# Three placements in a queued schedule: masks behind the token sums, bias preparation last, a longer pause ahead of the scaling

## The chip, the cores and the metric

The kernel runs on one core of a Trainium2 chip. The time is the device time of one execution in microseconds (us). The kernel before takes 2967.13 us (median of three runs, 2965.59 to 2967.64). A trace is one execution, and the same kernel's runs differ by 1 to 5 us, so a difference of a microsecond between two traces is not by itself an effect. The "granted clock" in the traces is the share of TensorE's full clock that it was given (1.00 is all of it).

## The reference, cut to what matters

```python
h = relu(layernorm(x))
for l in range(2):
    u_left, u_right = (h @ (h @ W[l].T).T / sqrt(768) for W in (W_left, W_right))
    u = u_left * triu(adj) + u_right * triu(adj, 1).T          # the masks
    e = exp(u) * adj
    attention = e / (e.sum(-1) + 1e-10)
    h_lin = h @ W_lin[l].T + b_lin[l]                          # bias, centred ahead of time
    h = relu(layernorm_ddof1(attention @ h_lin) * a[l] + b[l]) # "scaling" of tokens
x = x + h
```

There are 128 graphs of 64 tokens, 768 features, in fp32. The kernel works through them in 16 blocks of 512 tokens, in two passes per layer.

## The kernel before

A block of pass one consists of six projections (left and right weights, three column groups). Each projection is computed by seven products of six matmuls (a Strassen-like scheme), into the banks X, Y, Z and V of PSUM (the memory into which this kernel's matmuls write; here a bank is read out before it is used anew). The products read the tokens `ht`, four sums of tokens `ts` (T1 to T4, made by GpSimd), and sums of weights. After each product, one piece of side work is taken from a queue:

```python
def pump(n):
    for _ in range(n):
        f = queue.popleft() if queue else None
        if f is None and idle:
            f = idle.popleft()          # an empty piece gives a turn to the idle work
        if f is not None:
            f()
```

What a block does for the next one, and what it leaves to the end:

```python
def prepare(u):
    transpose_rows(l, u, sp)                       # norm, transposes, store to DRAM
    queue.append(lambda: load_h(1, l, u))          # ht back from DRAM
    if u + 1 < NB:
        queue.append(lambda: load_rows(l, u + 1, sp))
    queue.extend(softmax(u - 2) if u > 1 else [])
    queue.append(lambda: load_adj(u))              # the adjacency
    queue.extend(none * 6)                         # the pause
    affine(1, l, u)                                # ScalarE scales ht (layer 1 only)
    queue.append(lambda: masks(u))                 # GpSimd: wm <- adj * tri, waits for adj
    sums_t((1, l, u))                              # GpSimd: T1 to T4 of ht
...
late = [queue.pop() for _ in range(2)][::-1]       # T3 and T4
for k in range(2):
    for g in range(CH):
        project(u, k, g, ...)
        if k == g == 0 and u in aside:
            aside[u]()                             # block 1: one_aside
        if k == 1 and g == CH - 2:
            flush()
            queue.extend(none * 3 + late)
```

The idle work of pass one is started in each layer's second block (`u == 1`):

```python
def one_aside(l):
    def begin():
        load_w(l, "n")      # four weight loads: A11, A21, A22, A12
        bias(l)             # two loads at once; its VectorE piece goes into the idle work
        centre(l)           # idle: 2 empty, mean of A11 and A21 (VectorE), subtractions (GpSimd), ...
        sums_w(l, "n", nc.gpsimd, idle, 2)
    return begin
```

In the traces VectorE, ScalarE, GpSimd and the load queue execute their instructions in program order: one that waits holds those behind it (T1 at 80.03 us, behind masks that started at 78.67). The queue therefore decides what stands in front of what on VectorE, ScalarE, GpSimd and the load queue.

## Time and profile before

| | before |
|---|---|
| time, median | 2967.13 us |
| TensorE busy | 2906.3 us, 98% |
| waits of TensorE that the change can touch | 31.0 us |
| layer 0, second and third block | 71.48 and 61.89 us |
| layer 1, first and second block | 59.32 and 80.39 us |
| a block without a gap | 59.98 us |

The block times run from the first product of a block (X, left weights) to that of the next. They are the right unit here, because a wait of TensorE costs more than its own length. The lines behind this table are in the prediction below.

### The profile page before, as it was taken

What the parts mean: (1) busy time and instruction counts of PE and PEld (TensorE: products, weight loads), DVE (VectorE), ACT (ScalarE), POOL (GpSimd) and SP (SyncE); (2) the same over time, 40 slices, a digit from 0 to 9 for tenths busy, and PEclk for the clock granted to TensorE, in tenths of its full rate; (3) what the DMA queues carried; (4) which work ended last, traced back from release to release, by engine and by line L of the source; (5) the groups of instructions that cost most, each with busy time, mean ns of one, the idle gap of its engine ahead of it and who ended that gap; (6) DMA issues with size and microseconds to landing.
All of it is one profiled execution on the core that took longest, in us unless ns stands there. A gap on an engine that the chain in (4) does not pass through costs nothing.

```text
span 2965.4 us, 37443 instructions
## 1 busy us (share of the span) xinstructions
PE 2906.3 (98%) x14872; PEld 2243.7 (76%) x14872; DVE 1128.6 (38%) x2316; ACT 582.6 (20%) x1113; POOL 754.4 (25%) x478
## 2 busy tenths in 40 slices
PE   8899999999999999999997999999999999999998
PEld 7788888888888655555586888888888886555554
DVE  5444334443343232222333333333333324555555
ACT  2112111211121122222211111111111112232221
POOL 0231111111211262322312211111111114656564
PEclk9999999999999999999998999999999999999999
DMA  6423432243222243332443342234223303554544
GB/s 191 115 70 81 115 83 70 73 112 94 70 70 72 103 134 120 100 118 94 141 116 94 103 104 71 70 91 114 74 70 86 101 24 114 169 160 148 177 143 133
DMA packets 228655, 310.23 MB, mean 105 GB/s; under 512 B 53632, under 2 KB 179072, under 8 KB 220288
## 3 DMA queue, kind: packets, MB, share of 16 engines
q1 hardware_dynamic: 228192, 307.05, 37.2%
q8 instruction: 117, 1.92, 0.3%
q10 hardware_dynamic: 288, 0.79, 0.1%
q14 instruction: 58, 0.48, 0.0%
HBM read 202.91 MB, written 104.86 MB: 104 GB/s over the span
## 4 chain that ended last, share of the span: by engine, by line
PE 94%; DMA 3%; DVE 1%; SPq 1%; issue 0%; ACT 0%; POOL 0%; DVEq 0%; ACTq 0%; POOLq 0%
PE Z L326 16%; PE V L326 16%; PE X L326 16%; PE Z L566 8%; PE V L566 8%; PE X L566 8%; PE Y L326 8%; PE aux L360 6%; PE Y L566 5%; PE aux L494 3%; DMA h<-xb 1%; DMA x<-z 1%; DMA x<-in_x_dram 0%; DMA b<-in_b_lin_dram 0%; SPq L273 0%
## 5 line engine op out<-in xcount | busy, mean ns | idle before, releaser
L296 POOL TENSOR_TENSOR wm<-adj,tri 128x256 f32<-128x256 f32 x64 | 46.3, 744 | 1423.9 <-DMA adj<-in_adj_dram 1225.2
L151 POOL TENSOR_TENSOR ts<-ht 128x768 f32<-128x768 f32 x126 | 240.1, 1906 | 284.4 <-PE Y L326 155.4
L326 PE MATMUL X<-ht,w_r_A 128*128 128x256 f32 x1152 | 281.1, 380 | 2.9 <-ACT n L345 2.9
L326 PE MATMUL V<-ts,w_l_A 128*128 128x256 f32 x1152 | 281.1, 380 | 0.0
L326 PE MATMUL X<-ht,w_l_A 128*128 128x256 f32 x1152 | 280.1, 379 | 0.0
L326 PE MATMUL V<-ts,w_r_A 128*128 128x256 f32 x1152 | 280.0, 379 | 0.0
L566 PE MATMUL X<-w_n_A,ht 128*128 128x384 f32 x768 | 268.8, 486 | 0.0
L566 PE MATMUL V<-w_n_A,ts 128*128 128x384 f32 x768 | 268.6, 486 | 0.0
L345 ACT COPY n<-X 128x256 f32<-128x256 f32 x192 | 71.4, 372 | 981.0 <-PE X L326 981.0
L347 DVE TENSOR_TENSOR n<-V,u 128x256 f32<-128x256 f32 x384 | 161.8, 421 | 235.9 <-PE V L326 235.3
L326 PEld LDWEIGHTS X<-ht,w_r_A 128*128 128x128 f32 x1152 | 219.4, 191 | 33.2 <-ACT n L345 3.3
L326 PEld LDWEIGHTS V<-ts,w_l_A 128*128 128x128 f32 x1152 | 219.8, 191 | 30.1
L326 PEld LDWEIGHTS X<-ht,w_l_A 128*128 128x128 f32 x1152 | 218.7, 190 | 30.3 <-issue 0.6
L326 PEld LDWEIGHTS V<-ts,w_r_A 128*128 128x128 f32 x1152 | 218.9, 190 | 29.8
L151 POOL TENSOR_TENSOR ts<-ht,ts 128x768 f32<-128x768 f32 x126 | 238.7, 1894 | 8.4 <-issue 6.0
L566 PEld LDWEIGHTS V<-w_n_A,ts 128*128 128x128 f32 x768 | 145.9, 190 | 101.8
L566 PEld LDWEIGHTS X<-w_n_A,ht 128*128 128x128 f32 x768 | 145.8, 190 | 101.6 <-issue 0.3
L340 DVE TENSOR_TENSOR u<-Y,s 128x256 f32<-128x256 f32 x192 | 81.4, 424 | 369.1 <-PE Y L326 362.1
L520 ACT ACTIVATE z<-aux 128x768 f32<-128x768 f32 x128 | 102.5, 806 | 597.9 <-PE aux L494 583.8
L347 DVE TENSOR_TENSOR n<-Z,u 128x256 f32<-128x256 f32 x192 | 81.4, 424 | 307.3 <-PE Z L326 307.2
L343 DVE TENSOR_TENSOR u<-Z,u 128x256 f32<-128x256 f32 x192 | 81.5, 424 | 280.5 <-PE Z L326 280.1
L337 ACT COPY s<-X 128x256 f32<-128x256 f32 x192 | 71.1, 370 | 587.0 <-PE X L326 586.9
(107 smaller groups left out, 3987.5 us busy)
## 6 DMA issues: line engine op xcount, KB each, us to landing
ht<-h SPq DMA_DIRECT2D x63, 1536.0 KB, 7.0
h<-xb SPq DMA_DIRECT2D x124, 384.0 KB, 6.1
z<-z SPq DMA_DIRECT2D x128, 192.0 KB, 2.9
x<-z SPq DMA_DIRECT2D x128, 192.0 KB, 8.7
xr<-in_x_dram SPq DMA_DIRECT2D x128, 192.0 KB, 3.4
out_dram<-xr SPq DMA_DIRECT2D x128, 192.0 KB, 2.7
x<-in_x_dram SPq DMA_DIRECT2D x120, 192.0 KB, 8.5
adj<-in_adj_dram SPq DMA_DIRECT2D x64, 128.0 KB, 2.8
```

Of the source, the lines that this page charges most:

```text
L151: eng.tensor_sub(b[o], b[m], b[n])
L296: nc.gpsimd.tensor_tensor(WM[u][:, :, k], ADJ[u][:, :, 1 - k], t, op=ALU.mult)
L326: nc.tensor.matmul(p, w[a][:, c, g * P:(g + 1) * P], b[t][:, c, :], start=(new and c == 0), stop=(c == CH - 1), skip_group_check=True)
L337: nc.scalar.copy(s1, p)
L340: nc.vector.tensor_add(u2, p, s1)
L343: nc.vector.tensor_add(u4, p, u2)
L345: nc.scalar.copy(to, pb)
L347: nc.vector.tensor_add(to, pb, (u4 if i == 3 else u2).rearrange("p (b s) -> p b s", s=S))
L360: nc.tensor.matmul(p[h * S:(h + 1) * S, q, :], ht[:, c, b * S:(b + 1) * S], m[c // CH][:, c % CH, b].rearrange("p k j -> p (k j)"), start= ...
L494: nc.tensor.matmul(cx[k][i, m, :HH], at[j, q, :], hl[j, q, m * HH:(m + 1) * HH], start=True, stop=True)
L520: nc.scalar.activation(zs[k].rearrange(two, n=2), cx[k], AF.Square, accum_out=ss[:, k:k + 1])
L566: nc.tensor.matmul(p, b[t][:, c, r * P:(r + 1) * P], w[a][:, c, :], start=(new and c == 0), stop=(c == CH - 1), skip_group_check=True)
```

## The change

The masks had GpSimd wait for the adjacency while the token sums stood behind them; they move to the end of the block. The bias preparation had VectorE wait for the bias; it moves behind the rest of the idle work. The scaling had ScalarE wait for `ht`; the pause ahead of it grows from six to nine empty pieces where a layer's second block is prepared, which happens during its first.

```diff
@@ prepare(u) @@
                 queue.append(lambda: load_adj(u))
-                queue.extend(none * 6)
+                queue.extend(none * (6 if u > 1 else 9))
                 affine(1, l, u)
-                queue.append(lambda: masks(u))
                 sums_t((1, l, u))
@@ end of a block @@
                             flush()
                             queue.extend(none * 3 + late)
+                            if u + 1 < NB:
+                                queue.append(lambda: masks(u + 1))
@@ one_aside(l) @@
             load_w(l, "n")
-            bias(l)
             centre(l)
             sums_w(l, "n", nc.gpsimd, idle, 2)
+            bias(l)
```

## The prediction

> **What bounds the kernel now.** I read the page's busy times first, then who waits for whom on TensorE, then busy time stretch by stretch, and only then the order of time around each wait.
>
> ```profile
> PE 2906.3 (98%) x14872; PEld 2243.7 (76%) x14872; DVE 1128.6 (38%) x2316; ACT 582.6 (20%) x1113; POOL 754.4 (25%) x478
> ```
>
> TensorE is busy 98% of 2965.4 us, and the diff removes no matmul. Only its idle time and its slow time are to be had. The waits of TensorE:
>
> ```profile
> PE Z L326 <- DVE u L343: 17.4, 2, 16.7
> ...
> PE Y L326 <- POOL ts L151: 9.0, 1, 9.0
> PE X L326 <- ACT n L345: 2.9, 1, 2.9
> PE aux L360 <- DVE n L347: 1.7, 1, 1.7
> ```
>
> Columns are total us, times, longest. These four make 31.0 us (the others, 14.1 us, are the start and a pass's edge, untouched). A wait also costs time afterwards, so I take whole blocks, from one block's first product to the next one's. The stretches below are layer 0's second, third and fourth block, then layer 1's first, second and third:
>
> ```profile
> 73.31:144.79 71.48, 62.48 (x349) 54.60 (x348) 29.23 (x67) 10.35 (x19) 14.11 (x11) 0.93 0.45 122
> 144.79:206.68 61.89, 60.23 (x350) 53.02 (x349) 28.57 (x60) 11.42 (x20) 18.46 (x11) 1.00 0.33 83
> 206.68:266.66 59.98, 59.98 (x350) 53.02 (x349) 23.59 (x56) 11.42 (x20) 18.91 (x12) 1.00 0.34 86
> 1478.89:1538.21 59.32, 56.45 (x254) 49.05 (x253) 16.08 (x35) 12.27 (x25) 12.28 (x10) 0.97 0.52 129
> 1538.21:1618.60 80.39, 63.00 (x349) 54.64 (x348) 29.70 (x56) 10.41 (x20) 16.26 (x10) 0.89 0.36 98
> 1618.60:1678.58 59.98, 59.98 (x349) 53.02 (x348) 19.14 (x42) 9.13 (x19) 19.60 (x11) 1.00 0.33 86
> ```
>
> Second column is the stretch, third PE busy, third from the end the granted clock. A full block takes 59.98 us with no gap. A layer's first has no scores (5.39 us in the chain of waits), so 54.59. The excess: 71.48-59.98 = 11.50; 61.89-59.98 = 1.91; 59.32-54.59 = 4.73; 80.39-59.98 = 20.41. In all 38.6 us, 1.3% of the time. That is the ceiling of this change: 2% (59 us) is out of reach.
>
> **What the Trainium skill says.** "Perfetto Trace Analysis", section "Optimization Strategy", says to find the gaps on the engine that limits and what blocks them; here the gaps name POOL, ACT and DVE, each itself held by a transfer. "TensorE: Matmul & The Clock Gate", section "What's actually happening", says that TensorE falls to half clock after an idle window and needs some 3.4 us of work to get back. The trace agrees: six matmuls of one product take 1.46 us in the steady state, after the 9.00 us pause 2.93; even the 2.87 us pause is followed by 2.62 and 2.13. So a wait costs about 2 to 2.6 us beyond its length (11.50-9.00 = 2.5), except one under 2 us (1.91-1.66). "SBUF — State Buffer", section "Who interferes with whom", says that a VectorE instruction with two SBUF inputs, or in a two-port mode, is shut out by a GpSimd instruction for its whole length. The trace agrees: the three-column add and scaling of the weight means take 0.16 and 0.17 us alone, but 1.62 and 1.74 at 146.68 and 148.34, ending where a GpSimd instruction ends (148.28, 150.04).
>
> **The change part by part.** A block runs six projections of seven products, 1.295 us apart (72.01 to 73.31). After each product one piece of the queue is given out; an empty piece takes one from the idle work. Engines work in program order, so a piece that waits for a transfer holds what follows.
>
> *Masks behind the token sums.* Layer 0's second block needs T2 for its second product (Y). In time:
>
> ```profile
> 63.31 0.35 SPq L211 DMA_DIRECT2D ht<-h  x1
> ...
> 73.31 1.46 PE L326 MATMUL X<-ht,w_l_A 128*128 128x256 f32 x6
> ...
> 78.67 1.40 POOL L296 TENSOR_TENSOR wm<-adj,tri 128x256 f32<-128x256 f32 x2 [49.51 <-DMA adj<-in_adj_dram]
> 80.03 1.80 POOL L151 TENSOR_TENSOR ts<-ht 128x768 f32<-128x768 f32 x1
> 81.91 1.80 POOL L151 TENSOR_TENSOR ts<-ht,ts 128x768 f32<-128x768 f32 x1
> ```
>
> The masks wait for the adjacency, and T1 and T2 stand behind them. Their data is there long before: ht is issued at 63.31 and takes 6.8 us to land, so 70.11. Without the masks ahead, T1 and T2 take the 3.7 us they take now (80.03 to 83.71) and end near 73.85; Y would start at 73.31+1.30 = 74.61. Margin 0.75 us. T3 and T4 follow by 77.5, before V needs T3 (some 82.5, behind the scores). All of 11.5 goes. The masks' consumer, the softmax, comes a block later. In the other blocks GpSimd's wait for the adjacency (1225.2 us over 27 waits) is beside TensorE and its end is worth nothing.
>
> *Longer pause.* Only a layer's second block gets nine empty pieces instead of six, given out during the first block. In layer 0 nothing is scaled, and the queue's rest is flushed at the same place, so there it does nothing. In layer 1 ScalarE's scaling waits for ht until 1516.46, and the copy that frees bank X, due at 1512.87, stands behind it until 1517.89. Three pieces later the scaling follows that copy; the next X product starts at its time (1515.26). The next copy then is delayed to about 1518.3, but its bank is needed only at 1520.4. T1 and T2 still end by 1523, needed at about 1535. So 4.7 goes.
>
> *Bias at the end of the idle work.* In layer 1's second block VectorE stands in the bias from 1562.5 to 1582.01, and TensorE stops at 1568.56:
>
> ```profile
> 1569.30 3.00 SPq L100 DMA_DIRECT2D w_n_A<-in_w_lin_dram  x4
> 1572.85 1.19 SPq L450 DMA_DIRECT2D b<-in_b_lin_dram  x2
> ...
> 1582.01 0.55 DVE L460 TENSOR_REDUCE bm<-b 128x1 f32<-128x384 f32 x1 [19.45 <-DMA b<-in_b_lin_dram]
> ...
> 1585.25 2.93 PE L326 MATMUL Z<-ht,w_l_S 128*128 128x256 f32 x6 [16.69 <-DVE u L343]
> ```
>
> But the next idle piece is the weights' mean, and it reads the weights whose loads were issued just ahead of the bias. Counting pieces: the bias had the first empty piece of the third projection; the mean now has the third. VectorE thus writes u (Y) and u (Z) at 1566.5, then waits for the first weight half: issued 1569.30, 7.8 us, lands 1577.1. Reduction 1.34: 1578.4. Second: issued about 1570.05, 8.4 us, lands 1578.45; reduction to 1579.8, two small instructions to 1580.2, then the n (V) write to 1580.6. TensorE can run X and Z meanwhile and stops only at the last V, due at 1569.7, until 1580.65: 10.9 us instead of 16.7. Afterwards two slow products (2.72 and 2.46): that projection's end plus one product is at 1585.8, where it was 1591.7. Saved: 5.9. The later 0.7 us wait (second mean, blocked by GpSimd) goes as the mean gets another place: 0.8. Of 20.4 some 6.7 goes, 13.7 stays, with VectorE's n (V) as the new releaser.
>
> *A cost.* In layer 0's second block the second mean moves from after the last projection's sixth product to after its second. Of the old clock: it starts at 139.0, two reductions to 141.6; GpSimd meanwhile runs T3, T4 and the moved masks (139.8 to 144.8), so each of the two small instructions waits for one of them to end: about 143.4 to 144.2. The u (Z) write then ends near 144.2 and the product Z due at 142.21 is 1.7 to 2.5 us late. The old place cost 1.9; I put the new one at 2.4: 0.5 lost. The bias itself (2.3 us of VectorE) falls in a later block, landed long since, and costs nothing.
>
> Sum: 11.5 + 4.7 + 6.7 - 0.5 = 22.4 us; 2967.1 - 22.4 = 2944.7.
>
> **Rivals.**
> 1. *The bias's wait goes altogether* (the intent): 20.4 goes, about 2931. For: the group was named by the bias. Against: the weights' landing times above.
> 2. *The mean inherits the whole wait*, because it effectively waits for all four weight loads: the last, issued 1571.95, takes 9.5 us and lands at 1581.4; the saving is about 3 and the time 2948.5. Against: each load is its own transfer with its own landing time.
> 3. *T2 comes just too late*: the margin is 0.75 us. A miss of 1 us with part of the slow clock would leave 1 to 3: 2946 to 2948.
> 4. *The masks at the block's end shut VectorE out* in every steady block: 1.4 us thirty times. VectorE has work of 38%, and products have two to four products of slack, so I expect nothing; at the worst some us.
>
> **Range and chances.** The first two parts (16.2 us) rest on slack read directly; the mean's new wait may be off by 3 either way, the cost by 1.5, rival 3 adds up to 3. Repeated runs differ by 2 us (2965.59 to 2967.64). So 2939 to 2951. The ceiling rules out 2% faster; nothing found could lose 59 us.
>
> **What would show it.** Right: no TensorE wait for POOL ts, none for ACT n; layer 0's second block near 60.5 to 62 us, with its end or the third block showing a wait of 1.5 to 2.5 for VectorE; layer 1's first block 54.6; its second about 73.7, with one wait of some 11 us of product V for VectorE's n, while VectorE's mean reduction (the weights' line) shows a wait for the weights' transfer. The steady blocks stay at 59.98. Wrong: layer 1's second block near 60 (rival 1) or above 76 (rival 2), a wait for ts left, or steady blocks over 60.1.

## The result, and the profile after

The changed kernel takes 2943.91 us (median of six runs, 2943.57 to 2945.87), the kernel before 2967.39 us over its runs of both occasions. The ratio is 0.9922, with a 95% interval of 0.991 to 0.9935. A ratio is the mean time of one kernel's runs over that of the other's of the same rounds, so it is not quite the ratio of the quoted medians. By its interval it is a saving of 0.8%. The prediction was 2944.7 us.

The first line of busy times on the page of the changed kernel:

```profile
PE 2901.8 (99%) x14872; PEld 2241.3 (76%) x14872; DVE 1125.1 (38%) x2316; ACT 583.1 (20%) x1113; POOL 754.9 (26%) x478
```

The number of matmuls is the same; TensorE is busy 4.5 us less; in the blocks below fewer products run at the slow clock (mean granted clock of layer 0's second block 1.00 instead of 0.93, of layer 1's second 0.93 instead of 0.89). The waits of TensorE in the changed kernel (total us, times, longest):

```profile
PE V L325 <- DVE n L346: 11.8, 1, 11.8
PE Z L325 <- DVE u L342: 0.9, 1, 0.9
```

The waits for `ts` (9.0), for ACT (2.9), for VectorE's `u` in layer 1 (16.7 and 0.7) and for VectorE's `n` at layer 0's scores (1.7) are gone. Two that the kernel before did not have stand there: in layer 1 product V for VectorE's `n` (11.8), in layer 0 product Z for VectorE's `u` (0.9). (The other lines of that answer are the start of the kernel, 13.2 us, and 0.7 us at a pass's edge.) The same stretches as before, now layer 0's second and third block and layer 1's first, second and third (start and end, length, busy times, granted clock, DMA share, GB/s):

```profile
73.96:135.08 61.12, 60.25 (x350) 52.94 (x349) 30.29 (x64) 10.36 (x19) 20.66 (x15) 1.00 0.53 143
135.08:195.06 59.98, 59.98 (x350) 53.02 (x349) 23.59 (x56) 11.42 (x20) 19.36 (x11) 1.00 0.33 86
1467.35:1521.84 54.49, 54.49 (x254) 47.98 (x253) 16.09 (x35) 12.27 (x25) 12.30 (x10) 1.00 0.57 140
1521.84:1595.38 73.54, 61.78 (x349) 54.02 (x348) 24.67 (x50) 10.52 (x20) 14.54 (x9) 0.93 0.40 107
1595.38:1655.36 59.98, 59.98 (x349) 53.02 (x348) 21.26 (x48) 9.14 (x19) 21.33 (x12) 1.00 0.33 86
```

Against the kernel before that is 71.48 + 61.89 - 61.12 - 59.98 = 12.27 us in layer 0, 59.32 - 54.49 = 4.83 us and 80.39 - 73.54 = 6.85 us in layer 1; together 23.95. The spans differ by 2965.4 - 2942.2 = 23.2 us; most of the rest is that the second block of layer 0 happened to start 0.65 us later (73.96 against 73.31), in a part that the change does not touch. The steady blocks all stay at 59.97 to 59.98, so the moved masks cost nothing there.

Layer 0's second block in order of time (start, length, engine, line, operation):

```profile
70.85 1.80 POOL L151 TENSOR_TENSOR ts<-ht 128x768 f32<-128x768 f32 x1 [42.26 <-DMA ht<-h]
...
72.73 1.81 POOL L151 TENSOR_TENSOR ts<-ht,ts 128x768 f32<-128x768 f32 x1
...
75.25 1.46 PE L325 MATMUL Y<-ts,w_l_S 128*128 128x256 f32 x6
...
79.51 1.41 POOL L296 TENSOR_TENSOR wm<-adj,tri 128x256 f32<-128x256 f32 x2 [1.43 <-DMA adj<-in_adj_dram]
```

T1 now waits for its own data only (`ht`, issued at 63.97, landing after 6.8 us). T2 ends at 74.54, and product Y starts at 75.25 without a wait: a margin of 0.71 us. The masks still wait for the adjacency, but nothing that TensorE needs soon stands behind them.

The pause, in layer 1's first block. In the kernel before, the copy that frees bank X stood behind the scaling, which waited for `ht`:

```profile
1516.46 1.52 ACT L218 ACTIVATE ht<-ht,b_col,a_col 128x512 f32<-128x512 f32 x2 [8.41 <-DMA ht<-h]
1517.89 0.35 ACT L345 COPY n<-X 128x256 f32<-128x256 f32 x1
1518.29 2.62 PE L326 MATMUL X<-ht,w_r_A 128*128 128x256 f32 x6 [2.87 <-ACT n L345]
```

In the changed kernel the copy comes first, and the next X product does not wait:

```profile
1501.32 0.37 ACT L344 COPY n<-X 128x256 f32<-128x256 f32 x1 [4.81 <-PE X L325]
1503.71 1.46 PE L325 MATMUL X<-ht,w_r_A 128*128 128x256 f32 x6
1504.84 1.52 ACT L218 ACTIVATE ht<-ht,b_col,a_col 128x512 f32<-128x512 f32 x2 [3.15 <-DMA ht<-h]
```

Layer 1's second block in order of time:

```profile
1552.03 1.46 PE L325 MATMUL Z<-ht,w_l_S 128*128 128x256 f32 x6
...
1553.58 2.89 SPq L100 DMA_DIRECT2D w_n_A<-in_w_lin_dram  x4
...
1561.71 1.35 DVE L111 TENSOR_REDUCE wm<-w_n_A 128x3 f32<-128x1152 f32 x1 [11.64 <-DMA w_n_A<-in_w_lin_dram]
1563.12 1.35 DVE L112 TENSOR_REDUCE wm<-w_n_A 128x3 f32<-128x1152 f32 x1
...
1564.78 0.42 DVE L346 TENSOR_TENSOR n<-V,u 128x256 f32<-128x256 f32 x1
...
1565.25 2.93 PE L325 MATMUL V<-ts,w_l_A 128*128 128x256 f32 x6 [11.76 <-DVE n L346]
```

VectorE reaches the mean of the weights 3.5 us before their load has even been issued (1550.06 against 1553.58), waits 11.64 us for it, and the small write that frees bank V stands behind. That is where the rest of the 20.4 us excess went: a wait on the bias became a wait on the weights.

Behind it stands the order of the load queue. The program asks for these loads after the block's first projection, but the queue holds the store of the next block's tokens, the load of its `ht` and eight loads of rows ahead of them; the store waits for VectorE's transposes until 1534.14, and the weights are issued only 31.7 us after the block's start. In layer 0 the same loads are issued at 73.53, before the block starts, and nothing waits for them. Issuing them earlier in layer 1 was not tried.

### The profile page after: what moved, and what is told of

The parts are those of the page before. It is cut to its first block, busy times and chain, and to the rows that moved or that the text cites. A ratio compares the mean times of both kernels' runs of the same rounds, so it can differ in the third digit from the quotient of the medians.

```text
span 2942.2 us, 37469 instructions
## 1 busy us (share of the span) xinstructions
PE 2901.8 (99%) x14872; PEld 2241.3 (76%) x14872; DVE 1125.1 (38%) x2316; ACT 583.1 (20%) x1113; POOL 754.9 (26%) x478
## 4 chain that ended last, share of the span: by engine, by line
PE 97%; DMA 1%; DVE 1%; SPq 0%; issue 0%; ACT 0%; POOL 0%; DVEq 0%; POOLq 0%
PE Z L325 17%; PE V L325 17%; PE X L325 17%; PE Y L325 8%; PE Z L567 8%; PE V L567 8%; PE X L567 8%; PE aux L359 6%; PE Y L567 5%; PE aux L495 3%; DMA x<-z 0%; DMA w_n_A<-in_w_lin_dram 0%; DMA h<-xb 0%; DMA at<-att 0%; PE aux L257 0%
## 5 line engine op out<-in xcount | busy, mean ns | idle before, releaser
L325 PE MATMUL V<-ts,w_l_A 128*128 128x256 f32 x1152 | 281.4, 380 | 11.8 <-DVE n L346 11.8
L577 POOL TENSOR_TENSOR u2b<-u,b 128x384 f32<-128x384 f32 x64 | 63.9, 999 | 474.1 <-DVE u L575 443.4
```

Of the source, the lines that this page charges most:

```text
L325: nc.tensor.matmul(p, w[a][:, c, g * P:(g + 1) * P], b[t][:, c, :], start=(new and c == 0), stop=(c == CH - 1), skip_group_check=True)
L577: nc.gpsimd.tensor_add(u2b, u2, rows["b2"])
```

## The experiments

Seven kernels were run, all correct. The first four shared nine runs of the kernel before (median 2966.84 us), the next two nine (2968.28), the last one seven (2966.56). This table gives the block times in us from one trace of each; "before" in the last column is the median of the first four's occasion. The experiments follow one by one.

| | layer 0, 2nd | layer 0, 3rd | layer 1, 1st | layer 1, 2nd | time, median |
|---|---|---|---|---|---|
| before | 71.48 | 61.89 | 59.32 | 80.39 | 2966.84 |
| changed | 61.12 | 59.98 | 54.49 | 73.54 | 2943.91 |
| masks alone | 60.84 | 59.98 | 60.58 | 78.01 | 2953.23 |
| pause alone | 72.00 | 61.63 | 54.49 | 79.28 | 2961.35 |
| bias alone | 74.25 | 59.98 | 59.56 | 72.22 | 2964.09 |
| changed, mean late | 59.98 | 59.98 | 54.50 | 59.97 | 2928.78 |
| changed, pairs exchanged | 61.11 | 59.98 | 54.49 | 78.09 | 2948.05 |
| before, adjacency early | 59.98 | 62.18 | 58.72 | 80.70 | 2954.92 |
| changed, all late, bias first | 59.98 | 60.12 | 54.49 | 59.98 | 2929.03 |

**Masks alone** (e1_masks). The kernel before with:

```diff
-                queue.append(lambda: masks(u))
                 sums_t((1, l, u))
...
                             queue.extend(none * 3 + late)
+                            if u + 1 < NB:
+                                queue.append(lambda: masks(u + 1))
```

> The kernel before with only the masks moved behind the token sums. My theory: layer 0's second block loses its 9.0 us wait for ts (71.48 us to about 60 to 60.5), the third block's 1.66 us wait shrinks or moves, the 0.7 us wait late in layer 1's second block goes; the 2.9 us wait for ACT and the 16.7 us wait for VectorE (bias) stay. Time about 2953.5 us, a saving of 13 to 14. Rival (the masks were only named last; T2 waits for its own data or something else takes the place): a TensorE wait for ts stays and the saving is under 5 us.

Measured: 2953.23 us, ratio 0.9954 (0.9942 to 0.9967), a saving of 13.6 us. The wait for `ts` is gone, the waits for ACT (2.9) and for the bias (16.3) stay. The masks' place was the cause, and the rival falls. Layer 0's second block took 60.84 us, a little over the expected 60 to 60.5, with a wait of 0.46 us left. Layer 1's first block is 1.3 us longer than before with the same 2.9 us wait; TensorE's return to full clock took longer this time (see the end).

**Pause alone** (e2_pause). The kernel before with:

```diff
-                queue.extend(none * 6)
+                queue.extend(none * (6 if u > 1 else 9))
```

> The kernel before with only the longer pause. My theory: layer 1's first block goes from 59.3 to 54.5 us, nothing else moves, layer 0's blocks keep 71.5 and 61.9: about 2962.6 us, a saving of 4.8. Rival: the pause has an effect in layer 0 as well, or it needs the moved masks to be of use: layer 0's second block changes by over 1 us, or layer 1's first block keeps its wait.

Measured: 2961.35 us, ratio 0.9982 (0.997 to 0.9995), a saving of 5.5 us. Layer 1's first block falls to 54.49, and the wait for ACT is gone. In layer 0 the wait for `ts` is 9.3 us where it was 9.0 and the two blocks are 0.5 longer and 0.3 shorter: no effect there beyond the spread of the traces, as expected. Layer 1's second block is 1.1 us shorter (79.28), with a bias wait of 16.05 us instead of 16.69, where nothing else was expected to move. The pause needs no help from the moved masks.

**Bias alone** (e3_bias). The kernel before with:

```diff
-            bias(l)
             centre(l)
             sums_w(l, "n", nc.gpsimd, idle, 2)
+            bias(l)
```

> The kernel before with only the bias preparation moved to the end of the idle work. My theory: the weight mean takes over the wait, so layer 1's second block goes from 80.4 to about 73.5 us, with one wait of 11 to 12 us of TensorE for VectorE; in layer 0 the second mean falls behind GpSimd's backlog and costs 1 to 3 us more: about 2962.5 us, a saving of 4 to 7. Rival (the diff's intent: the bias alone held VectorE): layer 1's second block at about 60 us, the whole about 2947.

Measured: 2964.09 us, ratio 0.9993 (0.9979 to 1.0006). On its own this part is not clear of noise; the median is 2.75 us lower, below what I expected. Layer 1's second block went to 72.22 us, as the theory has it, with a wait of 10.2 us (11 to 12 expected); the rival's 60 us falls. But 8.2 us gained there were partly given back. Layer 0's second block grew by 2.8 us while the third lost 1.9: the second mean stood behind GpSimd's backlog (a 2.00 us scaling that takes 0.17 alone, and a 1.71 us wait of TensorE); the rest of the growth lies at the wait for `ts` (9.2 us) and the slow clock after it. And layer 1's third block, 59.98 before, took 61.28 us. There the bias itself met GpSimd, which the waits and order of time of this run show:

```profile
1667.75 1.82 POOL L151 TENSOR_TENSOR ts<-ht,ts 128x768 f32<-128x768 f32 x1
...
1667.92 2.06 DVE L464 TENSOR_TENSOR b<-b,b 128x384 f32<-128x384 f32 x1
...
1670.83 1.56 PE L326 MATMUL Z<-ht,w_r_S 128*128 128x256 f32 x6 [1.04 <-DVE u L343]
```

The subtraction of the two bias halves took 0.55 us in the kernel before; here it took 2.06, beside a GpSimd instruction. This is what the Trainium skill, "SBUF — State Buffer", section "Who interferes with whom", says of a VectorE instruction with two SBUF inputs beside a GpSimd one that reads SBUF. In the changed kernel the bias comes 51.5 us into that block instead of 54.1; its subtraction takes 0.55 us, and the block takes 59.98. The traced run is the fastest of the five (2961.92 us), and its blocks save 5.8 us, so the trace does not account for a median that saves only 2.75. The three savings taken alone add up to 13.6 + 5.5 + 2.75 = 21.9 us by the medians and to 13.7 + 5.7 + 5.8 = 25.1 by the blocks of the traces; the change saves 23.5 and 23.95. Within that uncertainty it is the sum of its parts; whether the parts act on each other is not shown.

**The mean late** (e4_late_mean). The changed kernel with two empty pieces ahead of the mean in layer 0 and nine in layer 1:

```diff
+            idle.extend(none * (2, 9)[l])
             centre(l)
             sums_w(l, "n", nc.gpsimd, idle, 2)
             bias(l)
```

> The changed kernel with the weight mean put later as well (2 empty pieces ahead of it in layer 0, 9 in layer 1). My theory: the wait of 11.8 us is only VectorE reaching the mean before the weights land; with the mean some 13 us later both waits go, layer 1's second block 73.5 to 60.0 us, layer 0's second 61.1 to 60.0: about 2929.2 us. Rival: another transfer or engine takes the wait over (the scaled tokens, the token sums), or the later mean delays the weight sums: layer 1's second or third block stays over 62 us and the time over 2932.

Measured: 2928.78 us, ratio 0.9872 (0.9859 to 0.9885) against the kernel before. The blocks in question have no gap left. Layer 0's second and layer 1's second block in this run:

```profile
73.64:133.62 59.98, 59.98 (x349) 53.02 (x348) 26.64 (x60) 10.36 (x19) 18.63 (x13) 1.00 0.55 146
...
1520.37:1580.34 59.97, 59.97 (x349) 53.01 (x348) 21.83 (x46) 10.41 (x20) 10.36 (x7) 1.00 0.48 132
```

TensorE's only waits left are the start and 0.4 us at a pass's edge. The first mean in layer 1 starts 1570.53 - 1520.37 = 50.2 us into the block, 22 us later than VectorE reached it in the changed kernel (more than the 13 us that I had put down). So the 11.8 us wait was VectorE reaching the mean before its loads had landed, no other transfer or engine took it over, and this version is faster than both kernels: by 1.3% against the kernel before.

**The pairs exchanged** (e5_swap). The changed kernel, with the first mean reading the fourth and third load:

```diff
-        for a, b in (("A11", "A21"), ("A12", "A22")):
+        for a, b in (("A12", "A22"), ("A11", "A21")):
```

> The changed kernel with the two pairs of weight halves exchanged in the mean, so that the first mean needs the fourth and the third load instead of the first and the second. My theory: the mean waits for exactly the loads it reads, so TensorE's wait in layer 1's second block grows by the later landing of the fourth load, from 11.8 to about 14.5 to 15.5 us, the block from 73.5 to about 76.5 to 77.2, the time to about 2947. Rival (the mean waits for all four loads however it is ordered, or VectorE is held by something else): block and time unchanged, 73.5 and 2943.9.

Measured: 2948.05 us (four runs, 2947.35 to 2948.94); layer 1's second block took 78.09 us, and TensorE waited 15.0 us. In order of time:

```profile
1552.49 2.82 SPq L100 DMA_DIRECT2D w_n_A<-in_w_lin_dram  x4
...
1564.43 1.35 DVE L111 TENSOR_REDUCE wm<-w_n_A 128x3 f32<-128x1152 f32 x1 [15.00 <-DMA w_n_A<-in_w_lin_dram]
1565.70 1.34 DVE L112 TENSOR_REDUCE wm<-w_n_A 128x3 f32<-128x1152 f32 x1
```

The same four loads, the same bias, and the wait grew by 3.2 us: the mean waits for the loads that it reads. Counted from the block's start, the last load it needs was there at 1564.43 - 1521.20 = 43.23 us, where it had been 1563.12 - 1521.84 = 41.28; the rest is that both reductions now run after that landing. The rival falls. The time and the block are about 1 us above what I expected; the wait itself is inside. The prediction's second rival had put a mean that needs the fourth load at 2948.5 us.

**The adjacency early** (e6_early_adj). The kernel before, masks in their old place, but each layer's second block loads its adjacency ahead of `ht`:

```diff
+                if u == 1:
+                    queue.append(lambda: load_adj(u))
                 queue.append(lambda: load_h(1, l, u))
...
-                queue.append(lambda: load_adj(u))
+                queue.append(lambda: load_adj(u) if u > 1 else None)
```

> The kernel before, masks still ahead of the token sums, but the adjacency of each layer's second block loaded ahead of its ht and rows. My theory: GpSimd was held by the adjacency's landing, not by the masks' 1.4 us, so layer 0's second block loses its 9.0 us wait this way too: 71.5 to about 60.5 us, the time about 2955.5. Rival (the masks' place is what matters, or the transfers ahead only push ht back): a wait for ts of over 2 us stays and the time is over 2958.

Measured: 2954.92 us, ratio 0.9955 (0.9943 to 0.9968). Layer 0's second block took 59.98 us. The masks ran at 65.07, T1 at 70.96 and T2 ended at 74.66. So it was the landing of the adjacency that held GpSimd: in the kernel before, T1 started 9.9 us after its `ht` had landed (80.03 against 70.11), of which the masks' own work was 1.4 us. An earlier load and a later use save nearly the same time here (13.4 and 13.6 us), but not in the same blocks: with the early load the scores of layer 0's third block still wait 2.0 us for VectorE's `n`, and the block takes 62.18 us.

**The bias first, all late** (e7_bias_first). The late-mean version with the bias back ahead of the mean:

```diff
             idle.extend(none * (2, 9)[l])
+            bias(l)
             centre(l)
             sums_w(l, "n", nc.gpsimd, idle, 2)
-            bias(l)
```

> The version with the late mean, but with the bias preparation put back ahead of the mean, as in the kernel before (so the idle work starts 2 and 9 pieces later and keeps its old order). My theory: what counted was that VectorE reached the first piece that reads the loads before they had landed, not which piece it was; so the old order costs nothing once the start is late: layer 1's second block 60.0 us, time 2928 to 2931, the same as with the bias last. Rival: the bias ahead of the mean is a cost of its own (its six instructions, about 2.3 us, or a lock by GpSimd): a TensorE wait of over 1 us and a time over 2931.

Measured: 2929.03 us (four runs, 2928.14 to 2929.46), ratio 0.9875 (0.9858 to 0.9891), the same as with the bias last. So the order of the bias and the mean did not matter; the start of the idle work did.

## Why the prediction was right

The time (2944.7 predicted, 2943.9 measured) is right, and so is the mechanism of each of the three parts. Three terms had the wrong size, one of them the wrong sign: the blocks gave 23.95 us where 22.4 were predicted. That the time is off by only 0.8 us is in part luck; layer 0's second block happened to start 0.65 us later. Point by point:

- **Masks.** Shown by the trace, by the masks alone and by the early adjacency. The margin of T2 was predicted as 0.75 us and measured as 0.71.
- **Pause.** Predicted 4.7 us in layer 1 and nothing in layer 0; measured 4.83 in the changed kernel, and alone 59.32 to 54.49 with layer 0 unchanged.
- **Bias.** Predicted: 6.7 of 20.4 us go, because the mean inherits the wait; measured 6.85. Two terms of that sum were off and cancelled, by luck. The wait was predicted as 10.9 us and measured as 11.76, because the weight loads were issued 0.65 us later in the block (31.74 us after its start, against 1569.30 - 1538.21 = 31.09) and took 8.1 and 8.7 us instead of 7.8 and 8.4. And TensorE's slow time after the wait was taken over from the old trace as 2.6 us, but measured 73.54 - 59.98 - 11.76 = 1.8. The prediction's "about 2 to 2.6 us beyond its length" was too narrow already for the old trace: the same block there gives 80.39 - 59.98 - 16.69 - 0.70 = 3.0.
- **The cost in layer 0.** Predicted as an excess of 2.4 us, measured as 1.14 with a wait of 0.87. I had T3 start when product Z ends; it starts when Y ends, as these lines of the changed kernel show (GpSimd and VectorE beside each other):

```profile
127.71 1.82 POOL L151 TENSOR_TENSOR ts<-ht 128x768 f32<-128x768 f32 x1 [4.33 <-PE Y L325]
...
129.49 1.81 POOL L151 TENSOR_TENSOR ts<-ht,ts 128x768 f32<-128x768 f32 x1
...
130.70 0.62 DVE L113 TENSOR_TENSOR wm<-wm 128x3 f32<-128x3 f32 x1
131.25 1.41 POOL L296 TENSOR_TENSOR wm<-adj,tri 128x256 f32<-128x256 f32 x2
131.35 0.65 DVE L114 TENSOR_SCALAR wm<-wm 128x3 f32<-128x3 f32 x1
```

  Each of the two small instructions does wait for a GpSimd instruction (0.62 and 0.65 us, where they take 0.16 and 0.17 alone), but what they meet is the end of T4 and half of the masks' 1.41 us. So the 0.5 us counted as lost were in fact 0.77 us gained (1.91 - 1.14).
- **Rivals.** The first (the bias's wait goes altogether, 2931) is refuted by the changed kernel and, as to layer 1's second block, by the bias alone; the second (the mean waits for all four loads) by the exchanged pairs, the third (T2 too late) by the margin. The fourth (masks at the end of every steady block) by 59.98 us there.

## What to carry to other kernels

When an engine works in order, removing the wait that a profile names uncovers the next instruction in its queue; look up when *that* one's data lands before counting the gain. Here the named wait was 16.7 us, and the next one 11.8. What ended both waits was to start the dependent work later (22 us or seventeen products in layer 1: an idle piece comes round only where the queue has none of its own), and with that the reordering of the bias was not needed. Whether loading the weights earlier would do as well was not tried.

## What the Trainium skill lacked or had wrong

- "TensorE: Matmul & The Clock Gate", section "What's actually happening", says that TensorE goes cold after an idle window of about 3.4 us. Here shorter waits were enough. After 2.87 us (kernel before) the next two products of six matmuls took 2.62 and 2.13 us instead of 1.46; after 2.28 us (adjacency early) they took 2.91 and 1.84, at a granted clock of 0.51 and 0.77. Waits of 1.04, 1.66, 1.71 and 1.98 us were followed by no slow product.
- The same section has a warm-up of about 3.4 us, varying by half a microsecond. From the lengths and granted clocks of the products after a wait one can estimate how long TensorE ran at half clock here: about 3.1 us in the changed kernel after the 11.76 us wait (2.72 us at 0.50, then 1.51 at 0.86), but about 6.0 us in masks alone after a 2.90 us wait (2.72 at 0.50, 2.56 at 0.50, 1.61 at 0.79). So it does not go by the length of the wait. In block times, what a wait cost beyond its length was between 1.7 us (masks alone, after 16.32 us: 78.01 - 59.98 - 16.32) and 3.2 us (masks alone, after 2.90 us: 60.58 - 54.49 - 2.90); some 0.3 us of that comes without any slow product (1.14 - 0.87 in the changed kernel's layer 0). The page warns that the window runs freely; the spread over these runs is 1.5 us, as much as some of the effects studied here.
- "SBUF — State Buffer", section "Who interferes with whom", agrees with these runs: the VectorE add and subtraction with two SBUF inputs took 0.62 and 2.06 us beside GpSimd instead of 0.16 and 0.55, the scaling 0.65 and 2.00 instead of 0.17, and the reductions of 1.34 us over the weights were never longer than 1.35. It does not say what happens when GpSimd has several instructions in a row; here VectorE came in between two of them (in the lines above, 130.70 + 0.62 = 131.32, T4's end being 129.49 + 1.81 = 131.30), so a small instruction waits for one of them and not for the row.
- "Perfetto Trace Analysis", section "Optimization Strategy", says to find what blocks the gaps. It lacks the warning that an engine working in order can hide a second wait behind the first: 16.69 us on the bias became 11.76 us on the weights.
